# Two attention layers with a feed-forward: rests of two chunk pairs issued together, and another order of the first projections

## The chip, the cores and the metric

The kernel runs on one core of a Trainium2 chip, in one launch. The metric is the device time of that launch in microseconds, the median of the runs shown; lower is better. Engines: TensorE (PE; its weight loads are listed apart as PEld), VectorE (DVE), ScalarE (ACT), GpSimd (POOL) and SyncE (SP), which here only issues transfers.

## The reference

Two layers over x of 4 x 512 x 320 (batch, rows, features), with a context of 4 x 1601 x 192. Each layer is self-attention with 20 heads of 16, cross-attention to the context, and a gated feed-forward, all in fp32:

```python
h1 = _ln(x, n1_g, n1_b)
x = _attn(h1, h1, q1, k1, v1, o1_w, o1_b, heads) + x
h2 = _ln(x, n2_g, n2_b)
x = _attn(h2, context, q2, k2, v2, o2_w, o2_b, heads) + x
h3 = _ln(x, n3_g, n3_b)
proj = h3 @ ff_w1 + ff_b1
a, g = jnp.split(proj, 2, axis=-1)
ff = a * jax.nn.gelu(g, approximate=False) @ ff_w2 + ff_b2
return ff + x
```

`ff_w1` is 320 x 2560, `ff_w2` 1280 x 320.

## The kernel before

**Units.** The work is a list of units in a fixed order: for each layer, self-attention for every batch and each of five groups of four heads, the same for cross-attention, then one feed-forward unit per batch. There are 88 units, eight of them feed-forward (here counted 0 to 7 in their order: 0 to 3 in the first layer, 4 to 7 in the second). The kernel writes out its own order (`manual_schedule`): each engine runs its instructions in the order in which the Python code issues them, and waits on semaphores for data and for buffers.

**Side work.** Everything that is not a unit's own main work (projections of queries, keys and values for units to come, norms, output projections) lies as closures in chains with a cost and a due round. `steps` runs some of them at fixed points of the main work; `run(chain)` runs the head of one chain at once, `until(test, chain)` runs heads until the test holds. The maxima of a later unit's scores (`max_pairs`: two score matmuls, then a VectorE reduction) are given out in the same way by `giver`.

**PSUM.** There are eight banks: pool `ps_st` has four single banks (tag `st`), pool `ps_m` two double ones (tag `m`). Side work takes a single bank (`step_bank`, L337), except in the opening, where it takes a double one. A set of four maxima in the opening and in a feed-forward unit takes one double bank and two single ones (`banks`, L879 to L886).

**Feed-forward unit** (`ff_main`, L1158). The normed and transposed x (`hT`) has 320 features: two slabs of 128 and a rest of 64. The 1280 hidden features are ten chunks of 128. For a chunk, the value half (index 0) and the gate half (index 1) each need two full matmuls over 128 rows (`full`, L1182) and one over the 64 rows left (`rest`, L1194). The 64 rows are stored twice, so that the rest of the value half uses the upper 64 rows of the array and the rest of the gate half the lower 64, side by side. `gate` is a Gelu on ScalarE (L1200) and one VectorE operation (L1201). Chunks go in pairs: side work (`beside`), four full matmuls of the first chunk, side work, four of the second, then the four rests of both, then the two gates. A pair holds two single banks and one double bank. After the five pairs, the second product (`yps`, L1221) follows with four row tiles, each over ten chunks.

**Opening** (L1341 to L1377). Unit 0's norm is made, then the queries and keys of units 0 and 1 are projected (`queries`, L687; `keys`, L713). Each projection is twelve matmuls into one bank. For unit 0, ScalarE (L631) and VectorE (L629) put the bank into the head slots by turns; for all others ScalarE copies it (`qst`, `kst`) and GpSimd puts it into slots (L635). Then four rounds of unit 0's maxima follow (sps L891, reduced at L907), with one piece of unit 0's values (`vps`, L818) between two rounds. There are eight pieces of values: four for the first two groups, four for the others. After the maxima come unit 2's queries, a piece of values, `max_reduce` and `max_end` (the maxima are turned and sent into the query buffer by eight small transfers, L962, from SP, ScalarE and GpSimd), loads, unit 2's keys and three pieces of values. Then the main loop starts with unit 0's scores (`st`, L1062).

Of the kernel before, what the change touches and what calls it, by code (L numbers as in the profile page):

```python
# [9 lines left out]
F32 = mybir.dt.float32  # L10
# [9 lines left out]
FF = 4 * D  # L20
L = 2
EPS = 1e-5
P = 128
# [20 lines left out]
NHC = FF // P  # L44
# [4 lines left out]
FK = [(0, 0, P), (1, P, P)]  # L49
REST = D - 2 * P  # L50
# [16 lines left out]
def kernel(ctx: ExitStack, tc: tile.TileContext, x, context, ws, out):  # L67
# [18 lines left out]
    nc = tc.nc  # L86
# [9 lines left out]
    ps_st = ctx.enter_context(tc.tile_pool(name="ps_st", bufs=4, space=PSUM))  # L96
    ps_m = ctx.enter_context(tc.tile_pool(name="ps_m", bufs=2, space=PSUM))
# [8 lines left out]
    for b in range(2):  # L106
        k, o = (const.tile([P, 1], F32, name=f"{n}{b}") for n in ("keep", "ones"))
# [11 lines left out]
    for i in range(2):  # L119
        m = const.tile([P, SLOT], F32, name=f"nmax{i}")  # L120
# [25 lines left out]
    for b in range(2):  # L146
        k = const.tile([P, 1], F32, name=f"kept{b}")
# [5 lines left out]
    for b in range(2):  # L153
        rows = slice(b * GD, (b + 1) * GD)
# [20 lines left out]
    w1 = wpool.tile([P, 2, 2 * FF], F32, name="w1")  # L175
# [6 lines left out]
    w1r = wpool.tile([P, FF], F32, name="w1r")  # L182
# [121 lines left out]
    at = 0  # L304
# [23 lines left out]
    chains = {n: deque() for n in ("divide", "project", "slots", "norm", "context", "early", "proj", "values")}  # L328
# [6 lines left out]
    start = {"on": True, "both": False}  # L335

    def step_bank(shape, name):  # L337

        if start["on"] and start["both"]:
            return ps_m.tile([P, 2, 512], F32, tag="m", name=name)[:, 0]  # L340
        return ps_st.tile(shape, F32, tag="st", name=name)

    def warm(n):

        ps = step_bank([P, 512], "wps")
        for _ in range(n):
            nc.tensor.matmul(ps[:, : 4 * P], lhsT=ident, rhs=fill, start=True, stop=True)
# [4 lines left out]
    def add(chain, cost, f, due, ready=yes, soon=yes):  # L352
        chains[chain].append((cost if isinstance(cost, tuple) else (cost,), due, ready, soon, f))
# [15 lines left out]
    def run(chain):  # L369
        costs, _, ready, _, f = chains[chain].popleft()  # L370
        assert ready(), chain
        f()
        clock["credit"] -= sum(costs)
# [49 lines left out]
    def until(test, name):  # L423
        while not test():
            assert chains[name], name
            run(name)
# [210 lines left out]
    def add_proj(u):  # L637
        wq, wk = wq2 if u.cross else wq1, wk1
        chain = "early" if u.early else "proj"
# [13 lines left out]
        first = units[u.i - u.g]  # L653
# [27 lines left out]
        def queries(part):  # L681
            w = N // 2 // parts
            at = [i * (N // 2) + part * w for i in range(2)]
            ps = step_bank([P, 512], "qps")
            for k, _, n in DK:
                for i, to, gs in tiles:
                    nc.tensor.matmul(  # L687
                        ps[to, :w],
                        lhsT=wq[:n, k, gs],
                        rhs=first.hT[:n, k, at[i] : at[i] + w],  # L690
                        start=(k == 0),
                        stop=(k == 2),
                    )
            if u.i == 0:
                for i in range(2):
                    to_slots(u.qbuf, at[i], ps, w, i, False, kept)
            else:
                stage = two.tile([P, N // 2], F32, tag="stage", name="qst")
                nc.scalar.mul(stage[:, :w], ps[:, :w], DH**-0.5)  # L699
                for i in range(2):  # L700
                    to_slots(u.qbuf, at[i], stage, w, i, False)
            if part == parts - 1:
                u.q = u.qbuf
                first.made["q"] += 1
                u.qwhen = -9 if start["on"] else clock["round"]
# [73 lines left out]
        def add_queries():  # L779
            if u.g == 0 and u.cross:  # L780
                add(chain, 0.0, hold, due - 4, yes, lambda: "h" in u.own)
            for part in range(parts):
                add(chain, (0.05 + 0.427 / parts,) * 3, lambda part=part: queries(part), due - 2, unread)

        if not u.cross:
            add_queries()
            add(chain, (0.477,) * 3, keys, due, free)
        else:
            add(chain, 2.45, keys_of_context, keys_due, free)
            add_queries()  # L790
            for _ in range(HG):
                add(
                    "slots", 0.0, lambda: u.kslots and u.kslots.popleft()(), keys_due,
                    lambda: u.keyed, lambda: clock["slots"] > 0,
                )
# [149 lines left out]
    def max_reduce(u):  # L945
        if u.pm is not None:
            nc.vector.tensor_reduce(
                u.nm[:, : HG * NQ].rearrange("p (j t) -> p t j", t=NQ), u.pm, AX.X, ALU.max, negate=True
            )
# [97 lines left out]
    def round_of(scores, maxima):  # L1047

        then = [f() for f in scores] + [f() for f in maxima]
        for f in then:  # L1050
            f()
# [106 lines left out]
    def ff_main(u, give, nxt):  # L1158
        done = 0

        def beside(room, n):

            nonlocal done
            if room:
                for extra in give(done, True)[1]:
                    round_of([], extra)
            done += n
            if done == u.steps - 1 and nxt is not None and nxt.kind != "ff":
                max_reduce(nxt)
                max_end(nxt)  # L1170
            steps(True)
            for _ in range(n - 1):
                steps(False)

        hc = one.tile([P, 6, N], F32, tag="ctxT", name="hid")
        hid = [hc[:, i, :] for i in range(6)]

        hid += [kbuf[1][:, i * N : (i + 1) * N] for i in range(3)] + [kbuf[2][:, :N]]

        def full(c, i, ps):  # L1180
            for k, at, n in FK:
                nc.tensor.matmul(  # L1182
                    ps,
                    lhsT=w1[:, k, i * FF + c * P : i * FF + (c + 1) * P],
                    rhs=u.hT[:, k, :],
                    start=(k == 0),
                    stop=False,
                )
            return ps

        def rest(c, pss):
            for i, ps in enumerate(pss):
                rows = slice(i * REST, (i + 1) * REST)
                nc.tensor.matmul(  # L1194
                    ps, lhsT=w1r[rows, c * P : (c + 1) * P], rhs=u.hT[rows, 2, :], start=False, stop=True
                )

        def gate(c, pss):
            gl = prs.tile([P, N], F32, tag="pr", name="gl")
            nc.scalar.activation(gl, pss[1], AF.Gelu, bias=b1[:, NHC + c : NHC + c + 1])  # L1200
            nc.vector.scalar_tensor_tensor(hid[c], pss[0], b1[:, c : c + 1], gl, ALU.add, ALU.mult)  # L1201

        for c in range(0, NHC, 2):

            beside(True, 2)
            gates = ps_m.tile([P, 2, 512], F32, tag="m", name="fps")
            pss = []
            for i in range(2):
                if i:
                    beside(False, 2)  # L1210
                ps = ps_st.tile([P, 512], F32, tag="st", name="fps")
                pss.append([full(c + i, 0, ps), full(c + i, 1, gates[:, i])])
            for i in range(2):
                rest(c + i, pss[i])
            for i in range(2):
                gate(c + i, pss[i])
        ff_read.append(u)
        for t in range(NQ):
            ps = ps_st.tile([P, 512], F32, tag="st", name="yps")
            for c in range(NHC):  # L1220
                nc.tensor.matmul(  # L1221
                    ps[:, :D],
                    lhsT=hid[c][:, t * P : (t + 1) * P],
                    rhs=w2[:, c, :],
                    start=(c == 0),
                    stop=(c == NHC - 1),
                )
            nc.vector.tensor_tensor(xs[u.b][:, t, :], ps[:, :D], xs[u.b][:, t, :], ALU.add)
            if u.l == L - 1:
                dma(out=out[u.b, t * P : (t + 1) * P, :], in_=xs[u.b][:, t, :])  # L1230
            beside(True, 1)
        after(u)
# [35 lines left out]
    def left(v):  # L1268
        return sum(map(len, v.pairs))
# [75 lines left out]

    add_norms(0)
    add_proj(units[0])
    warm(5)
    add_proj(units[1])
    until(lambda: not chains["proj"], "proj")  # L1350
    add_values(units[0])
    add_proj(units[2])
    first = units[0]
    first.pairs = max_pairs(first)
    start["both"] = True
    while left(first):
        round_of([], first.pairs[0].popleft() + first.pairs[1].popleft())
        if left(first):
            run("values")

    run("proj")
    run("values")
# [9 lines left out]
    start["on"] = start["both"] = False  # L1372
    run("proj")

    for _ in range(3):
        run("values")
    clock["credit"] = 0.0  # L1377

# [45 lines left out]
```

## Time and profile before

| | |
|---|---|
| median of 3 runs | 3214.34 us (3212.0 to 3215.55) |
| profiled execution | 3212.79 us |
| span of its trace | 3211.0 us |
| granted TensorE clock, mean | 0.999 |

Busy time in us by stage, from the trace. The two feed-forward stages are the third and the fifth row.

| stage, us from the start | PE | DVE | ACT | POOL |
|---|---|---|---|---|
| opening, 0 to 34 | 28.30 | 20.53 | 8.52 | 18.45 |
| attention, layer 0, 34 to 1334 | 1285.00 | 963.40 | 942.21 | 564.10 |
| feed-forward, layer 0, 1334 to 1633 | 295.50 | 75.81 | 38.03 | 41.50 |
| attention, layer 1, 1633 to 2934 | 1288.80 | 947.07 | 944.33 | 559.98 |
| feed-forward, layer 1, 2934 to 3211 | 273.07 | 56.06 | 32.96 | 19.09 |

A row of the timeline gives the start, the busy time from first to last, the engine and source line, the operation, output and inputs by their names in the program (with buffer numbers left out), the sizes, and the count; in brackets stands how long the engine had been idle and what ended that. Adjacent instructions of one line are merged into one row. The profile counts two TensorE instructions (passes) for each matmul of the program. Ends of matmuls are modelled; the distances between starts are the safer reading.

### The profile page before, as it was taken

Reading aid. Unit: us, or ns where it says so; the run is one execution under the profiler, and the core shown is the slowest. Engines: PE = TensorE matmul, PEld = TensorE weight load, DVE = VectorE, ACT = ScalarE, POOL = GpSimd, SP = SyncE. Lnnn points to the kernel's source line nnn. Section 1 sums busy time; section 2 is a strip of 40 time slices with the busy share of each in tenths; the row PEclk is TensorE's granted clock in tenths of the full one; section 3 lists DMA queues with packets and bytes.
Section 4 is the critical chain, followed back from the end, with each engine's and each line's share of the span. In section 5 each row is a group of like instructions: output and inputs, shape, how many; then the busy total and the mean of one; then the engine's idle time right before and its main releaser. Section 6 shows DMA issues by size and latency. Waiting matters only on the chain.

```text
span 3211.0 us, 81827 instructions
## 1 busy us (share of the span) xinstructions
PE 3170.7 (99%) x33970; PEld 1465.7 (46%) x33970; DVE 2062.9 (64%) x2663; ACT 1966.1 (61%) x3951; POOL 1203.1 (37%) x1617
## 2 busy tenths in 40 slices
PE   9999999999999999999999999999999999999999
PEld 3444444444444444354444444444444444443555
DVE  7776877778778677422247778777777777773221
ACT  4666577777777777611146665777778777785110
POOL 4555234444443443211225553344444444442000
PEclk9999999999999999999999999999999999999999
DMA  2130011100100100100012100010010010001000
GB/s 67 48 78 17 14 24 40 33 21 19 33 21 20 31 16 11 39 6 0 1 30 56 38 14 14 21 29 16 16 31 11 16 33 10 15 10 37 9 11 15
DMA packets 104999, 77.94 MB, mean 24 GB/s; under 512 B 42924, under 2 KB 95156, under 8 KB 104628
## 3 DMA queue, kind: packets, MB, share of 16 engines
q1 hardware_dynamic: 104544, 72.70, 9.3%
q8 instruction: 268, 4.39, 0.6%
q14 instruction: 103, 0.84, 0.1%
q0 software_dynamic: 64, 0.00, 0.0%
q10 hardware_dynamic: 20, 0.00, 0.0%
HBM read 33.04 MB, written 7.93 MB: 13 GB/s over the span
## 4 chain that ended last, share of the span: by engine, by line
PE 63%; DVE 2%; POOL 1%; ACT 0%; issue 0%; DMA 0%; SPq 0%; POOLq 0%; DVEq 0%
PE st L1062 15%; PE av L1082 13%; PE fps L1182 9%; PE sps L891 8%; PE yps L1221 5%; PE fps L1194 2%; PE ops L1009 2%; PE kps L743 2%; PE qps L687 2%; PE vps L836 2%; PE sps L915 1%; PE vps L818 1%; PE kps L713 1%; PE hps L489 1%; DVE nmax L907 1%; DVE pm L907 1%
## 5 line engine op out<-in xcount | busy, mean ns | idle before, releaser
L1068 ACT ACTIVATE pr<-st 128x512 f32<-128x512 f32 (+1 forms) x2720 | 1412.7, 601 | 432.1 <-PE sps L891 349.0
L1062 PE MATMUL st<-q,kT 32*128 32x512 f32 (+1 forms) x5440 | 1374.4, 615 | 9.7 <-ACT pr L1068 5.7
L907 DVE TENSOR_REDUCE pm<-sps 128x2 f32<-128x1024 f32 (+1 forms) x974 | 1134.8, 1203 | 271.9 <-PE sps L891 265.8
L891 PE MATMUL sps<-kT,q 32*128 32x512 f32 x5120 | 1272.6, 620 | 14.3 <-DVE nmax L907 11.7
L1099 POOL TENSOR_TENSOR o<-o,vo 128x512 f32<-128x512 f32 x576 | 736.2, 1278 | 1389.0 <-ACT vo L1098 1248.3
L1062 PEld LDWEIGHTS st<-q,kT 32*128 32x128 f32 (+1 forms) x5440 | 511.3, 181 | 528.0 <-ACT pr L1068 309.3
L1082 PE MATMUL av<-pr,vals 128*32 128x512 f32 (+1 forms) x5440 | 730.4, 605 | 0.2
L907 DVE TENSOR_REDUCE nmax<-sps 128x2 f32<-128x1024 f32 (+1 forms) x339 | 378.4, 1157 | 155.9 <-PE sps L891 152.8
L891 PEld LDWEIGHTS sps<-kT,q 32*128 32x128 f32 x5120 | 408.5, 183 | 120.7 <-issue 79.3
L1098 ACT COPY vo<-av 128x512 f32<-128x512 f32 x576 | 347.4, 603 | 41.8 <-PE av L1082 37.8
L1082 PEld LDWEIGHTS av<-pr,vals 128*32 128x32 f32 (+1 forms) x5440 | 109.9, 108 | 495.3 <-ACT pr L1068 483.5
L1182 PE MATMUL fps<-hT,w 128*128 128x512 f32 x640 | 288.2, 599 | 1.1 <-DVE hid L1201 0.6
L1200 ACT ACTIVATE gl<-fps,b 128x512 f32<-128x512 f32 x80 | 50.7, 684 | 387.4 <-PE fps L1194 387.3
L635 POOL TENSOR_SCALAR q<-qst,keep,zero 64x128 f32<-64x128 f32 (+1 forms) x476 | 230.4, 484 | 48.6 <-ACT qst L699 15.4
L1182 PEld LDWEIGHTS fps<-hT,w 128*128 128x128 f32 x640 | 117.3, 190 | 148.6 <-issue 143.2
L1201 DVE SCALAR_TENSOR_TENSOR hid<-fps,b,gl 128x512 f32<-128x512 f32 x48 | 33.8, 746 | 163.1 <-ACT gl L1200 163.1
L1009 PEld LDWEIGHTS ops<-wo,aT 112*32 112x32 f32 (+1 forms) x3072 | 97.7, 110 | 68.4 <-issue 37.6
L687 PE MATMUL qps<-hT,wq 112*32 112x128 f32 (+3 forms) x2880 | 125.6, 308 | 0.5 <-DVE pm L907 0.5
L1009 PE MATMUL ops<-wo,aT 112*32 112x160 f32 (+1 forms) x3072 | 125.2, 300 | 0.2
L687 PEld LDWEIGHTS qps<-hT,wq 112*32 112x32 f32 (+1 forms) x2880 | 86.2, 110 | 79.0 <-issue 38.0
L437 POOL TENSOR_SCALAR root<-root 128x4 f32<-128x4 f32 x23 | 5.3, 230 | 309.4 <-DVE root L431 308.8
L502 POOL TENSOR_TENSOR x<-x,brow 128x320 f32<-128x320 f32 x96 | 84.0, 893 | 89.1 <-DVE hn L476 78.3
(88 smaller groups left out, 2182.4 us busy)
## 6 DMA issues: line engine op xcount, KB each, us to landing
kT<-kst SPq DMA_DIRECT2D x320, 48.0 KB
aT<-o SPq DMA_DIRECT2D x320, 32.0 KB
q<-turned SPq DMA_DIRECT2D x636, 1.0 KB
w<-in_L_xattn_ff_w_dram SPq DMA_DIRECT2D x20, 256.0 KB
ctxT<-ctxT SPq DMA_DIRECT2D x24, 208.0 KB
ctxT<-ctxT SPq DMA_DIRECT2D x12, 416.0 KB
ctxin<-in_ctx_dram SPq DMA_DIRECT2D x24, 192.0 KB
w<-in_L_xattn_ff_w_dram SPq DMA_DIRECT2D x20, 160.0 KB
```

Of the source, the lines that this page charges most:

```text
L635: nc.gpsimd.tensor_scalar(to, stage[rows, :w], keep[b][rows], more[rows], ALU.mult, ALU.add)
L687: nc.tensor.matmul(ps[to, :w], lhsT=wq[:n, k, gs], rhs=first.hT[:n, k, at[i] : at[i] + w], start=(k == 0), stop=(k == 2),)
L891: nc.tensor.matmul(ps, lhsT=u.q[j * SLOT : (j + 1) * SLOT, t * P : (t + 1) * P], rhs=u.kT[j * SLOT : (j + 1) * SLOT, u.k0 + s * 512 : u.k0 ...
L907: nc.vector.tensor_reduce(to[:, j : j + n], part, AX.X, ALU.max, negate=(ns == 1))
L1009: nc.tensor.matmul(ps[f : f + m, : D // 2], lhsT=aT[:n, k, t * P + f : t * P + f + m], rhs=wo[:n, k, cols], start=(k == 0), stop=(k == 2),)
L1062: nc.tensor.matmul(st[:r, :], lhsT=u.kT[rows, u.k0 + u.cols[c] : u.k0 + u.cols[c] + r], rhs=u.q[rows, :], start=True, stop=True)
L1068: nc.scalar.activation(p[:r], st[:r], AF.Exp)
L1082: nc.tensor.matmul(ps[i * SLOT : (i + 1) * SLOT, :], lhsT=columns_of[:r, head : head + SLOT], rhs=pr.pop((c, j))[:r, :], start=True, stop= ...
L1098: nc.scalar.copy(vo, ps)
L1099: nc.gpsimd.tensor_tensor(u.o, u.o, vo, ALU.add)
L1182: nc.tensor.matmul(ps, lhsT=w1[:, k, i * FF + c * P : i * FF + (c + 1) * P], rhs=u.hT[:, k, :], start=(k == 0), stop=False,)
L1221: nc.tensor.matmul(ps[:, :D], lhsT=hid[c][:, t * P : (t + 1) * P], rhs=w2[:, c, :], start=(c == 0), stop=(c == NHC - 1),)
```

## The change

There are three edits.

1. In `ff_main`, `rest` becomes `rests`, for a whole pair of chunks, and can come first or last. When a pair has not been begun ahead, its full matmuls run as before, then its rests, and directly behind them the banks of the next pair are taken and that pair's rests are issued, as the first matmuls of their sums (`start=True`). The gates of the first pair follow. The next pair then has only its full matmuls, the last of which closes the sums. With five pairs in a unit, pairs 1 and 3 are begun ahead; pair 4 is as before. The side work keeps its places: two points per pair.
2. In `add_proj`, unit 0's keys are added ahead of its queries; for all other units the order stays.
3. In the opening, unit 0's projections alone come before its maxima; unit 1's queries stand after the first round of maxima, its keys after the second, a piece of values after the third. After unit 2's keys, four pieces of values follow instead of three.

Apart from the rests, the opening and the work in it that these edits move, the instructions of every engine stand in the order of before. SP's and GpSimd's order does not change at all.

```diff
         if not u.cross:
-            add_queries()
+            if u.i:
+                add_queries()
             add(chain, (0.477,) * 3, keys, due, free)
+            if not u.i:
+                add_queries()
...
+        def full(c, pss, ahead):
+
             for i, ps in enumerate(pss):
+                for k, at, n in FK:
+                    nc.tensor.matmul(
+                        ps,
+                        lhsT=w1[:, k, i * FF + c * P : i * FF + (c + 1) * P],
+                        rhs=u.hT[:, k, :],
+                        start=ahead and k == 0,
+                        stop=not ahead and k == 1,
+                    )
+
+        def rests(c, pss, ahead):
+
+            for e in range(2):
+                for i, ps in enumerate(pss[e]):
+                    rows = slice(i * REST, (i + 1) * REST)
+                    nc.tensor.matmul(
+                        ps,
+                        lhsT=w1r[rows, (c + e) * P : (c + e + 1) * P],
+                        rhs=u.hT[rows, 2, :],
+                        start=ahead,
+                        stop=not ahead,
+                    )
...
+        def banks():
+            gates = ps_m.tile([P, 2, 512], F32, tag="m", name="fps")
+            return [[ps_st.tile([P, 512], F32, tag="st", name="fps"), gates[:, e]] for e in range(2)]
+
+
+        pss = None
         for c in range(0, NHC, 2):
...
+            ahead = pss is not None
+            if not ahead:
+                beside(True, 2)
+                pss = banks()
+
+            for e in range(2):
+                if e or ahead:
+                    beside(ahead and not e, 2)
+                full(c + e, pss[e], not ahead)
+            these, pss = pss, None
+            if not ahead:
+                rests(c, these, False)
+                if c + 2 < NHC:
+                    pss = banks()
+                    rests(c + 2, pss, True)
+            for e in range(2):
+                gate(c + e, these[e])
...
     warm(5)
+    until(lambda: not chains["proj"], "proj")
     add_proj(units[1])
-    until(lambda: not chains["proj"], "proj")
     add_values(units[0])
     add_proj(units[2])
     first = units[0]
     first.pairs = max_pairs(first)
     start["both"] = True
-    while left(first):
+    for chain in ("proj", "proj", "values", None):
         round_of([], first.pairs[0].popleft() + first.pairs[1].popleft())
-        if left(first):
-            run("values")
+        if chain:
+            run(chain)
...
-    for _ in range(3):
+    for _ in range(4):
         run("values")
```

More of the change, by code (lines that the diff above doesn't have):

```diff
@@ L1178, in ff_main @@
         hid += [kbuf[1][:, i * N : (i + 1) * N] for i in range(3)] + [kbuf[2][:, :N]]
[L1180 to L1191, printed above, removed]
-            for i, ps in enumerate(pss):
[L1193 to L1196, printed above, removed]
+        def full(c, pss, ahead):
+            for i, ps in enumerate(pss):
+                for k, at, n in FK:
[17 more added lines that the diff above has]
+                    )
         def gate(c, pss):
@@ L1201, in gate @@
             nc.vector.scalar_tensor_tensor(hid[c], pss[0], b1[:, c : c + 1], gl, ALU.add, ALU.mult)
+        def banks():
+            gates = ps_m.tile([P, 2, 512], F32, tag="m", name="fps")
+            return [[ps_st.tile([P, 512], F32, tag="st", name="fps"), gates[:, e]] for e in range(2)]
+        pss = None
         for c in range(0, NHC, 2):
[L1205 to L1216, printed above, removed]
+            ahead = pss is not None
[14 more added lines that the diff above has]
+                gate(c + e, these[e])
         ff_read.append(u)
```

## The prediction

> **What bounds the kernel.** I read the page's totals first, then the TensorE stream of the feed-forward stages in order of time, then the first 35 us on all engines.
>
> ```profile
> span 3211.0 us, 81827 instructions
> PE 3170.7 (99%) x33970; PEld 1465.7 (46%) x33970; DVE 2062.9 (64%) x2663; ACT 1966.1 (61%) x3951; POOL 1203.1 (37%) x1617
> PEclk9999999999999999999999999999999999999999
> ```
>
> TensorE is busy 3170.7 of 3211.0 us at the full clock. No work on it is removed: the built order of the changed program holds the same matmuls, and outside the start and the eight feed-forward units the order on every engine is as before. So the change can act only through what lies between matmuls: the price of switching between shapes, waits for a PSUM bank, and the start, where TensorE is not yet the bound.
>
> **The price of a switch.** The last feed-forward unit has nothing beside it (TensorE in order of time: start, duration, line):
>
> ```profile
> 3149.91 7.13 PE L1182 MATMUL fps<-hT,w 128*128 128x512 f32 x16
> 3156.98 1.99 PE L1194 MATMUL fps<-hT,w1r 64*128 64x512 f32 x8
> 3158.89 7.13 PE L1182 MATMUL fps<-hT,w 128*128 128x512 f32 x16
> ```
>
> The profile shows two passes per matmul. Rows of L1182 with 8 and 16 passes last 3.70 and 7.13 us elsewhere, so a pass takes 3.43 / 8 = 0.429 us. L1194's two 64-row halves run side by side: 8 passes count as 4. A period is 3158.89 - 3149.91 = 8.98 us, and 20 x 0.429 = 8.57; the 0.41 left is two switches, **0.205 us each**. A switch hides nothing and is hidden by nothing while TensorE is the bound.
>
> **Part 1, the rests.** Before, every pair of chunks runs F8 R4 (8 full matmuls, 4 rests), with other work before the first and between the two F4. After, pairs 1 and 3 of a unit (counted from 0) have their rests run directly behind those of pairs 0 and 2: R8, later F8 with no R4. Counted in the two built orders, switches from a unit's first L1182 to its last rest and the work behind it are, unit by unit, 18, 11, 10, 26, 18, 13, 10, 10 before (116) and 15, 7, 6, 24, 15, 10, 6, 6 after (89). 27 x 0.205 = **-5.5 us**.
>
> [...] The row is of this very switch, so I take -5.5.
>
> **What the open pair costs.** [...] There are four single banks and two double ones; a pair holds two singles and a double, so at R8 two open pairs hold all. Work directly behind R8 must wait for the gates of the first. [...] The rows give the price (VectorE, ScalarE, TensorE around one rest of unit 3):
>
> ```profile
> 1584.59 1.99 PE L1194 MATMUL fps<-hT,w1r 64*128 64x512 f32 x8
> 1586.65 1.27 ACT L1200 ACTIVATE gl<-fps,b 128x512 f32<-128x512 f32 x2 [5.09 <-PE fps L1194]
> 1587.37 1.41 DVE L1201 SCALAR_TENSOR_TENSOR hid<-fps,b,gl 128x512 f32<-128x512 f32 x2 [9.37 <-ACT gl L1200]
> 1588.17 0.86 PE L818 MATMUL vps<-wv,hT 112*32 112x128 f32 x24 [0.53 <-DVE hid L1201]
> 1588.69 2.41 DVE L907 TENSOR_REDUCE nmax<-sps 128x2 f32<-128x1024 f32 x3
> ```
>
> Let R be the start of the rests. The Gelu starts at R + 2.06, and a matmul that waits for the first gate's bank starts at R + 3.58 (1588.17 - 1584.59). The second bank comes one gate, 0.67, later: R + 4.25. R8 itself lasts 8 x 0.429 + 0.205 = 3.63. So whoever needs one bank finds it free (3.58 < 3.63): **0** for five of the nine (output projections, keys, a lone transpose), with 0.05 to spare. The built order's waits show ScalarE released by the fourth rest, not the eighth.
>
> At one place in unit 3, three banks are asked for: R8, maxima (sps), then values (vps), where the values' only bank is the one a maximum has just been written to. VectorE must finish both gates (R + 4.2), then reduce the double bank, whose scores start at R + 3.63 and are readable about 1.25 later as at the start (17.74 to 18.99), so R + 4.88; plus 1.2 and 0.6 (the 2.41 row is 1.2 + 0.6 + 0.6) and a 0.07 release: values at R + 6.75. Before they stood at R + 3.58; adding the 1.71 of the four extra rests gives 5.29. **+1.5 us**. Queued behind that wait on TensorE is everything; nobody else is late.
>
> At three places the three transposes of the next norm (hps) stand behind a rest, and before, the third of them or the full matmuls behind already wait for the first gate:
>
> ```profile
> 1435.44 1.99 PE L1194 MATMUL fps<-hT,w1r 64*128 64x512 f32 x8
> 1437.36 1.09 PE L489 MATMUL hps<-ident,hn 128*128 128x128 f32 x8
> 1439.03 0.66 PE L489 MATMUL hps<-ident,hn 128*128 128x128 f32 x4 [0.58 <-DVE hid L1201]
> 1439.52 7.10 PE L1182 MATMUL fps<-hT,w 128*128 128x512 f32 x16
> ```
>
> From rest to full matmul that is 4.08. After: first transpose at R + 3.63, second at 4.25 (second gate), third when ScalarE has copied the first (after both Gelus; 0.72 a copy): about 5.0, full matmuls at 5.5. Less the 1.71 moved in: 3.8, a gain of 0.3 in units 1 and 2. In unit 6 (rest at 3097.41, full matmuls at 3101.00: 3.59) only two transposes follow: 4.25 + 0.49 - 1.71 = 3.0, a gain of 0.55. Together **-1.15**.
>
> Where R8 is followed by F (unit 7, and the first R8 of most), the banks are held already and nothing waits. Part 1: -5.5 + 1.5 - 1.15 = **-5.15 us**.
>
> **Part 2, the start.** TensorE is idle for long here; the end is set by evacuations, then by maxima on VectorE, then by small transfers:
>
> ```profile
> 17.13 0.55 DVE L629 TENSOR_SCALAR kT<-kps,keep,ones 64x256 f32<-64x256 f32 x1 [0.63 <-ACT kT L631]
> ...
> 17.74 1.24 PE L891 MATMUL sps<-kT,q 32*128 32x512 f32 x8 [0.30 <-DVE kT L629]
> ...
> 18.99 9.78 DVE L907 TENSOR_REDUCE nmax<-sps 128x2 f32<-128x1024 f32 x12 [1.30 <-PE sps L891]
> ...
> 30.80 1.30 POOL L962 DMA_DIRECT2D q<-turned  x2
> ...
> 34.08 0.70 PE L1062 MATMUL st<-q,kT 32*128 32x512 f32 x2 [1.35 <-ACT vals L825]
> ```
>
> ScalarE and VectorE empty two banks, queries then keys, each in four alternating steps (13.61 to 17.68 us, a step every 0.58). The first maxima need all keys but only the first half of the queries. With keys first, the last two steps are no longer waited for: 17.74 - 2 x 0.58 = 16.57. VectorE's own last step still ends at 17.68, just ahead of the first scores at 16.57 + 1.25 = 17.82. Unit 1's projections, 24 passes each (L687 and L713 take 1.3 to 1.45), had cost nothing before: they ran under the evacuations. Now they stand between the maxima, 1.43 + 1.17 for the scores = 2.60 against VectorE's 2.45 (9.78 / 4): 0.15 lost twice. The values they displace (0.86) fitted. So the last maximum ends 1.17 - 0.3 = **0.9** earlier. From there on all is queued as before: POOL copies unit 2's queries (2.48) ahead of its two transfers, which the first scores at 34.08 wait for, and both hang on the query projection behind the last maxima: it moves with them. The four values then behind the keys take at most 2 x 0.8 + 2 x 1.0, ending before 33. The sixth values now stand among unit 2's maxima, where VectorE works without a pause (9.53 us in 11 reductions from 40.93): 0; if TensorE were the bound there, +1.0. SP's transfers keep their order. **-0.9 us**, from -1.2 to +0.1.
>
> **Sum.** -5.15 - 0.9 = -6.05 on the profiled execution: 3212.79 to 3206.7 with the span from 3211.0 to 3205.0. Its own time lies 1.55 below the median; on the median, 3214.34 - 6.1 = **3208.2**.
>
> **Rivals.**
> - The gates come later than the rows say (slower). If ScalarE were released only when all eight rests are through, each of the nine places pays 1.7 more: 15.4 - 6.1 = +9.3, **3223.6**. It decides from 0.7 us a place (6.1 / 9). For it: 3.58 against 3.63 is a margin of 0.05, and at unit 3 one wait is real. Against: the wait is on the fourth rest. 0.08.
> - The start gives nothing and the edges cost a little more (0.1 at each of the nine): -6.1 + 0.9 + 0.9 = -4.3, **3210.0**. For it: the first scores wait for a chain that includes POOL and transfers. 0.24.
> - More is gained: the wait in unit 3 is not met, because the values find another bank: -7.6, **3206.7**. Against it: the waits of the built program. 0.18.
> - That the change does not do what it says is excluded by the built order.
>
> My forecast has 0.50, with 3206.5 to 3210 around it.
>
> **Range and chances.** Down to the larger gain with the start at its best (3214.34 - 7.9 = 3206.4), less 1.8 for the scatter of the three runs shown (3212.0 to 3215.55): 3204.6. Up to the smaller gain plus 1.8: 3212. Less than 0.2%, 6.4 us, is about what a measurement of this kernel cannot tell from no change, so the line lies at 3207.9, just under my forecast. Faster: the larger gain (0.18) and a little over half of the forecast (0.28), 0.46. Same: the rest of the forecast (0.22) and the smaller gain (0.24), 0.46. Slower: 0.08.
>
> **What would show it.** Right: in the last unit, rests of 16 passes whose successor starts 3.63 us later, and three of them instead of five; a wait of about 1.5 us before the values in unit 3, and none of note behind the other R8; the first maxima at 17.8 and the first scores at 33.1; the two feed-forward stages shorter by 5 us together. Wrong: waits for a gate of 0.5 us or more behind most R8, a first score still near 34, or a gain that turns up in the attention stages, which nothing here touches.

## The result, and the profile after

| | before | after |
|---|---|---|
| median | 3213.99 us (22 runs, 3210.83 to 3218.35) | 3208.68 us (22 runs, 3205.31 to 3212.6) |
| ratio, 95% interval | | 0.9982 (0.9975 to 0.9988) |
| span of the profiled execution | 3211.0 us | 3209.2 us |
| granted TensorE clock, mean | 0.999 | 0.997 |

The change takes 5.3 us off (3.9 to 8.0 by the interval). The prediction's sum was 6.05, and its time 3208.2.

The page of the changed kernel has as many instructions as before on every engine, and nearly the same busy time of TensorE (busy us, share of the span, instructions):

```profile
PE 3170.0 (99%) x33970; PEld 1470.0 (46%) x33970; DVE 2064.1 (64%) x2663; ACT 1965.7 (61%) x3951; POOL 1201.8 (37%) x1617
```

The two profiled spans differ by only 1.8 us. Where the other 3.5 went is seen by stage, with a second profile of the changed kernel (after_again, below) beside the first. Each boundary is the start of a TensorE row: the first scores, the first full matmul of a feed-forward stage, the first scores of layer 1.

| stage, us | before | after | after_again |
|---|---|---|---|
| opening | 34.08 | 33.42 | 31.87 |
| attention, layer 0 | 1300.00 | 1298.86 | 1298.79 |
| feed-forward, layer 0 | 301.74 | 301.74 | 301.73 |
| attention, layer 1 | 1292.56 | 1295.90 | 1295.75 |
| feed-forward, layer 1 | 282.62 | 279.28 | 279.26 |

Feed-forward of layer 1 is 3.34 shorter. That of layer 0 has not changed at all. The opening differs by 1.55 between two executions of the same program. And the attention of layer 1, which the change doesn't touch, is 3.34 and 3.19 longer in the two profiles of it. The rows explain each.

**Layer 1.** The last unit on TensorE (start, duration, line, sizes, passes):

```profile
3146.98 3.70 PE L1200 MATMUL fps<-hT,w1r 64*128 64x512 f32 x16
3150.61 14.00 PE L1187 MATMUL fps<-hT,w 128*128 128x512 f32 x32
3164.54 3.70 PE L1200 MATMUL fps<-hT,w1r 64*128 64x512 f32 x16
```

The rests come as 16 passes, their successor 3.63 later, and nothing waits: two pairs cost one stretch of rests instead of two.

**The open pair.** In unit 1 the transposes behind the rests are released nearly as forecast (TensorE):

```profile
1432.70 3.70 PE L1200 MATMUL fps<-hT,w1r 64*128 64x512 f32 x16
1436.34 1.27 PE L489 MATMUL hps<-ident,hn 128*128 128x128 f32 x8
1437.87 0.66 PE L489 MATMUL hps<-ident,hn 128*128 128x128 f32 x4 [0.26 <-ACT hT L496]
```

The full matmuls follow at 1438.36, which is 3.95 behind the rests without the 1.71 of the four rests moved in (forecast 3.8, before 4.08). Only the third transpose shows a wait, 0.26, for ScalarE's copy of the first.

Unit 3 is where layer 0 loses again what it gains:

```profile
1579.99 3.70 PE L1200 MATMUL fps<-hT,w1r 64*128 64x512 f32 x16
1583.62 1.73 PE L894 MATMUL sps<-kT,q 32*128 32x512 f32 x8
1586.68 0.86 PE L821 MATMUL vps<-wv,hT 112*32 112x128 f32 x24 [1.32 <-DVE nmax L910]
1587.47 5.35 PE L1187 MATMUL fps<-hT,w 128*128 128x512 f32 x8
```

The values stand at R + 6.69 (forecast R + 6.75), behind the wait for the maximum that was foreseen. Then comes what was not: the next eight full passes take 5.35 instead of 3.70. The windows of 5 us (busy time by engine, then the granted clock, the DMA share and GB/s) show why:

```profile
1585.00:1590.00 5.00, 3.68 (x28) 1.77 (x28) 3.36 (x7) 0.27 (x1) 0.00 (x0) 0.74 0.02 3
1590.00:1595.00 5.00, 5.00 (x32) 2.08 (x31) 0.00 (x0) 0.37 (x1) 0.13 (x1) 0.92 0.00 0
```

The clock fell, to 0.74 and 0.92 as means of these windows. The trace's own record of the clock has it at 0.50 for 3.41 us, from 1587.42 on. Half of that, 1.71, is about the 1.65 that the eight passes lose.

**The opening** of the profiled run has the same loss. TensorE, VectorE and GpSimd in order:

```profile
16.55 1.42 PE L894 MATMUL sps<-kT,q 32*128 32x512 f32 x8 [1.71 <-DVE q L629]
17.90 2.79 PE L687 MATMUL qps<-hT,wq 112*32 112x256 f32 x24
18.06 2.42 DVE L910 TENSOR_REDUCE nmax<-sps 128x2 f32<-128x1024 f32 x3 [0.38 <-PE sps L894]
...
21.82 7.37 DVE L910 TENSOR_REDUCE nmax<-sps 128x2 f32<-128x1024 f32 x9 [1.34 <-PE sps L894]
...
31.22 1.30 POOL L965 DMA_DIRECT2D q<-turned  x2
...
33.42 0.70 PE L1065 MATMUL st<-q,kT 32*128 32x512 f32 x2
```

The first scores for the maxima start at 16.55 (forecast 16.57). The clock record has the next fall from 17.29 on, and unit 1's queries take 2.79 instead of 1.50, so VectorE waits 1.34 for its second round, and the maxima end at 29.19: 0.4 later than before, not 0.9 earlier. Still the first score is 0.66 earlier, since it now comes 2.20 behind GpSimd's transfers, and came 3.28 behind them (34.08 - 30.80). So one loss was not foreseen (the clock), and one gain (the transfers).

### The profile page after: what moved, and what is told of

Read it like the earlier page. It is cut to its first block, busy times and chain, and to the rows that moved or that the text cites. A ratio compares the mean times of both kernels' runs of the same rounds, so it can differ in the third digit from the quotient of the medians.

```text
span 3209.2 us, 81827 instructions
## 1 busy us (share of the span) xinstructions
PE 3170.0 (99%) x33970; PEld 1470.0 (46%) x33970; DVE 2064.1 (64%) x2663; ACT 1965.7 (61%) x3951; POOL 1201.8 (37%) x1617
## 3 DMA queue, kind: packets, MB, share of 16 engines
q8 instruction: 268, 4.39, 0.6%
## 4 chain that ended last, share of the span: by engine, by line
PE 64%; DVE 2%; POOL 1%; ACT 0%; issue 0%; DMA 0%; SPq 0%; POOLq 0%; DVEq 0%
PE st L1065 16%; PE av L1085 13%; PE fps L1187 9%; PE sps L894 8%; PE yps L1241 5%; PE fps L1200 2%; PE ops L1012 2%; PE kps L743 2%; PE qps L687 2%; PE vps L839 2%; PE sps L918 1%; PE hps L489 1%; PE vps L821 1%; PE kps L713 1%; DVE nmax L910 1%; DVE pm L910 1%
```

## The experiments

**The two halves alone.** `rests_only` has the new feed-forward and the old opening; `start_only` the reverse. The edits are the two halves of the change's diff; of the second:

```diff
+    until(lambda: not chains["proj"], "proj")
     add_proj(units[1])
...
-    while left(first):
+    for chain in ("proj", "proj", "values", None):
```

> The rests of two pairs together, the opening as before. Theory (27 switches fewer at 0.205 us, 1.15 gained at the transposes, 1.5 lost at the bank wait in unit 3 and 1.7 more there because the clock falls to half for one window of 3.4 us after that wait): -5.5 - 1.15 + 1.5 + 1.7 = -3.5 us against the kernel before. Rival (the clock's fall in unit 3 was chance): -5.2. Rival (the gain of the whole change comes from the opening): 0. The trace should show the values in unit 3 about 6.7 us after the rests, and full matmuls behind them at 5.3 us for 8 passes if the fall belongs to the wait, 3.7 if it was chance.

> The new opening, the feed-forward as before. Theory (the gap of 1.7 us before the first maxima halves TensorE's clock for one window, which eats 1.4 of what keys first gain): -0.7 to -1.5 us against the kernel before, with the query projection of unit 1 again at about 2.8 us instead of 1.5. Rival (the fall in the opening was chance): -2, the projection at 1.5, the last maximum at about 27.8. Rival (the opening carries the gain of the whole change): -5.

Measured: `rests_only` 3209.69 (21 runs), ratio 0.9991 (0.9984 to 0.9997), 3.8 below the median of before; `start_only` 3212.23 (13 runs), ratio 0.9993 (0.9985 to 1.0001), 1.2 below. Together -5.0, against -5.3 for the whole: the halves add up, and neither is nothing, though for `start_only` alone the interval reaches just past 1. In `rests_only` unit 3 shows the same wait of 1.32, and the clock falls there too: behind it the values take 1.21 instead of 0.86, and the eight full passes 5.00 instead of 3.70.

**The rests of unit 3 left as before, the rest of the change kept.**

```diff
-                if c + 2 < NHC:
+                if c + 2 < NHC and (nxt is None or nxt.kind == "ff"):
```

`nxt` is the unit behind; only unit 3 has an attention unit there.

> The whole change, but in feed-forward unit 3, the one with maxima beside it, every pair is as before. Theory: the bank wait of 1.5 and the fall of the clock (1.7) go, two switches (0.4) come back: 2.8 us faster than the whole change, so about -8 against the kernel before, and unit 3 lasts 63.6 us from its first transpose to the second product instead of 66.1. Rival (that wait costs nothing in the end, because the attention units behind make it up): as the whole change, -5.3.

Measured: 3204.97 (7 runs), ratio 0.9973 (0.9962 to 0.9985): 8.5 below the kernel before as measured beside it; the change was 5.3 below. In unit 3 the rests start at 1579.91 and the values 3.59 later, as before (TensorE):

```profile
1583.50 0.87 PE L821 MATMUL vps<-wv,hT 112*32 112x128 f32 x24 [0.53 <-DVE hid L1211]
1584.29 3.70 PE L1187 MATMUL fps<-hT,w 128*128 128x512 f32 x8
```

The feed-forward of layer 0 is 299.18 instead of 301.74, 2.56 shorter. So reordering unit 3, which saves two switches, costs 2.56 net where the clock falls.

**Two dummy matmuls in the gap before the first maxima.**

```diff
     start["both"] = True
+    warm(2)
```

> The whole change, with two more matmuls of no use (identity by a constant tile, 4 passes, 1.7 us) put into the gap before the first maxima; nothing else is altered. Theory (idle TensorE halves its own clock): unit 1's query projection takes 1.5 us instead of 2.8, the maxima end at 27.8 instead of 29.2, the first scores stand 1.4 earlier: 1.4 us faster than the whole change, -6.7 against the kernel before. Rival (the projection is slow for another reason, say an operand that comes late): no faster, or 0.2 slower for the added passes.

In its opening the dummies run from 14.57 to 16.55; behind the first scores come (TensorE and VectorE):

```profile
17.55 1.51 PE L687 MATMUL qps<-hT,wq 112*32 112x256 f32 x24
17.73 9.84 DVE L910 TENSOR_REDUCE nmax<-sps 128x2 f32<-128x1024 f32 x12 [0.26 <-PE sps L894]
```

With the gap filled the queries take 1.51 and the twelve reductions run through; the first score is at 31.80, 1.62 earlier than in the change's first profile. The time is 3208.09 (12 runs), ratio 0.9983 (0.9975 to 0.9992): 5.4 below before where 6.7 was expected, and no different from the change. Its profile gives a second reading that was not planned: unit 3 has the same wait of 1.32, and no fall behind it.

```profile
1585.06 0.86 PE L821 MATMUL vps<-wv,hT 112*32 112x128 f32 x24 [1.32 <-DVE nmax L910]
1585.85 3.70 PE L1187 MATMUL fps<-hT,w 128*128 128x512 f32 x8
```

Its layer-0 feed-forward is 300.08: the wait alone costs 300.08 - 299.18 = 0.90, the fall 301.74 - 300.08 = 1.66.

**The change again**, for a second profile.

> The change itself once more, for a second profile and beside the other three on one chip. Theory (a fall of the clock follows a gap of TensorE of 1.3 to 1.7 us, if the gap and the windows of the clock lie so that enough of one window is idle): the opening's fall is there again between 15 and 25 us; the fall in unit 3 behind the 1.32 wait is there or not. Time -5.3 against before, as in the first comparison; u3_warm 4 less than it. Rival (the falls are chance, wherever they come): no fall in the opening.

Measured: 3208.76 (16 runs), ratio 0.9983 (0.9976 to 0.9991). In the opening the rival was right, for this execution: the same gap, no fall, and maxima without a pause from 17.80 to 27.64 (TensorE and VectorE):

```profile
16.55 1.14 PE L894 MATMUL sps<-kT,q 32*128 32x512 f32 x8 [1.71 <-DVE q L629]
17.62 1.50 PE L687 MATMUL qps<-hT,wq 112*32 112x256 f32 x24
17.80 9.84 DVE L910 TENSOR_REDUCE nmax<-sps 128x2 f32<-128x1024 f32 x12
```

In unit 3 the clock fell, as in the first profile. Counted over the profiles that have the bare gap of 1.71 in the opening, it fell in three of six (`after`, `start_only`, `no_ahead_u3`; not in `after_again`, `no_ahead_again`, `fetch_after`); behind unit 3's 1.32 in three of five (`after`, `after_again`, `rests_only`; not in `warm_gap`, `fetch_after`). Whether it comes differs from one execution to the next; the last section shows from the clock records what decides it at these two places.

**Both losses mended**, with dummies, or with work that is needed anyway in the gap:

```diff
     start["both"] = True
-    for chain in ("proj", "proj", "values", None):
+    run("values")
+    for chain in ("proj", "proj", None, None):
```

> The whole change, with unit 3 left in the old order of rests (as in no_ahead_u3), and two matmuls on numbers that nobody reads in the gap before the first maxima (as in warm_gap). Theory (two separate losses of the change, each mended by itself): 1.6 less than no_ahead_u3 in its profile at the first score, so about 3203.5 where no_ahead_u3 gave 3205.0, and some -9.5 to -10 against before. Rival (the clock fall in the opening only moves: the windows of the clock run on, and a fall saved here comes elsewhere): the same as no_ahead_u3, -8.5. Rival (the gap of unit 3 was chance in one run of rounds): as warm_gap, -5.4.

> As u3_warm, but what fills the gap before the first maxima is work that is needed anyway: the first piece of unit 0's values comes there, instead of between the third and the fourth round of the maxima. Theory (the clock falls because TensorE stands still for 1.7 us): the piece fills about 0.9 to 1.3 of the gap, no fall, TensorE's queue behind it is 0.9 shorter than in u3_warm, but the maxima are VectorE's and end at the same time or 0.3 later, since VectorE or another engine copies the piece out; so first score at 31.8 to 32.4 and the time within 0.6 of u3_warm. Rival (a gap of 0.5 to 0.8 that stays is enough for a fall): maxima at half speed as in the change, first score at 33.1 to 33.6, the time that of no_ahead_u3.

Measured: `u3_warm` 3206.49 (9 runs), ratio 0.9975 (0.9965 to 0.9984); `u3_values` 3204.82 (7 runs), ratio 0.9974 (0.9963 to 0.9984). No gain over `no_ahead_u3` is seen, though the first score in these two profiles is at 31.80 and 31.54 instead of 33.08. In those profiles the clock fell twice in the attention of layer 0, in that of `no_ahead_u3` once. Once more, on one chip:

> The change with unit 3 left in the old order (as no_ahead_u3), once more for a narrower interval, beside the next kernel. Theory (the loss of unit 3 is 0.9 in the wait and 1.7 in a fall of the clock behind it, in some 3 of 5 executions): 0.9973 again, 2 to 3.5 better than the change's 0.9982; the bare gap of 1.7 us in the opening brings a fall or not. Rival (the first seven runs were lucky): 0.998 to 0.9985.

> The same with a piece of values in the gap before the first maxima (as u3_values), once more. Theory (the filled gap saves a fall worth 1.55 in some 3 of 5 executions, and falls elsewhere are chance): about 1 us less than no_ahead_again. Rival (a fall saved in the opening comes at one of the later standstills instead): the same time within the interval.

Measured: 3207.06 (5 runs), ratio 0.9965 (0.9953 to 0.9978), and 3206.37 (6 runs), ratio 0.9967 (0.9955 to 0.9979). The runs of the kernel before fell into two groups here, around 3213 and 3220, so these ratios support the first ones and don't sharpen them; the two kernels beside each other can't be told apart. The filled gap buys nothing that these runs can measure. Whether a fall saved in the opening comes later, or the saving is lost in the scatter of chance falls, is open.

**The price of a switch, by a dose the other way.** In the kernel before, each chunk's rests directly behind its own full matmuls: 69 switches more.

```diff
                 pss.append([full(c + i, 0, ps), full(c + i, 1, gates[:, i])])
-            for i in range(2):
                 rest(c + i, pss[i])
```

> The kernel before, with the rests of a chunk issued right behind that chunk's own four full matmuls instead of one stretch for the pair. Nothing else is changed. A feed-forward unit then switches more often between full passes and passes of 64 rows: 185 switches in the eight units instead of 116, 69 more. [...] Against it stands that the first chunk's gate starts four full matmuls earlier, so that the edge waits at the banks of the units with side work, 0.5 to 0.6 each, may shrink by up to 3.3. So +9 to +14, likeliest +11. Rival (a switch costs nothing, and the gain of the rests in the change came from the gates' timing): earlier gates, so 0 or down to -3. Rival (the price is only paid on one edge of a stretch of rests): +5 to +7.

Measured: 3227.68 (5 runs), ratio 1.0043 (1.0030 to 1.0055), 14.1 above before. The last unit:

```profile
3156.43 3.70 PE L1182 MATMUL fps<-hT,w 128*128 128x512 f32 x8
3160.07 1.13 PE L1194 MATMUL fps<-hT,w1r 64*128 64x512 f32 x4
3161.12 3.70 PE L1182 MATMUL fps<-hT,w 128*128 128x512 f32 x8
```

A chunk takes 3161.12 - 3156.43 = 4.69, a pair 9.38, against 8.98 in the kernel before: 0.40 for two switches more. From the first full matmul of a stage to the scores behind it (layer 0), or to the last row of the second product (layer 1), the stages are 6.46 and 7.04 longer, 13.50 / 69 = 0.196 a switch. Rivals of nothing and of one edge alone fall. The edge waits gave back much less than the 3.3 allowed for them.

**The transfers.** What made them land sooner in the new opening? The rate of all DMA from 27 to 36 us, in 40 slices of 0.225 us, first in the kernel before, then in the changed one:

```profile
GB/s 0 0 0 0 0 0 0 0 0 0 0 0 0 0 5 0 5 0 5 1 76 5 5 5 1 17 114 182 336 86 51 119 267 359 336 330 171 250 232 241
```

```profile
GB/s 0 0 0 0 0 0 0 0 0 73 0 0 0 0 0 0 5 2 2 0 5 3 1 5 5 5 0 40 165 239 279 245 370 319 347 256 262 234 180 174
```

The peak that stands alone (76, 73) is a fetch of 16 KB of instructions. The profile's page counts 268 on that queue, 4.39 MB, one for every 127 of TensorE's 33970 passes, or 254 instructions with the weight load of each pass (127 is the count where the expectation of `fetch_before` says 128). Whose instructions they are is read by stage: in the kernel before, the four stages behind the opening have 123, 10, 124 and 8 fetches, one for 127, 131, 126 and 129 passes of TensorE, but for 16, 6, 15 and 6 instructions of ScalarE and 10, 17, 9 and 16 of VectorE. So they are taken for TensorE's. Before, the lone fetch lies at 31.5 us, inside the flight of GpSimd's transfers (issued at 30.80); after, at 29.0, ahead of it. That suggested a test: more but narrower dummy matmuls at the very start move every fetch 27 matmuls forward in the work. In the old opening this takes a fetch out of the flight; in the new one it brings the next fetch in.

```diff
-    warm(5)
+    warm(32, 76)
```

> The kernel before; only the five dummy matmuls of 512 columns at the very start are 32 of 76 columns, about as long together. TensorE's instruction stream has 27 matmuls more, so each fetch of its instructions (one for every 128 passes, 16 KB) comes 27 matmuls earlier in the work. Before, a fetch lay at 31.5 us, inside the flight of GpSimd's two small transfers (issued at 30.80, landed 2.9 us later). Theory (a fetch of TensorE's instructions in that flight holds the transfers up by about 1 us): the fetch now comes at about 29, ahead of the flight; issue to landing 1.9 instead of 2.9, first score 1.0 earlier against the end of the maxima (4.2 to 4.3 us behind it instead of 5.3), time about -1. Rival (the flight is shorter with the new order for another reason, the state of SP's queue or of the copies): 2.9 to 3.5 as in all profiles of the old opening.

> The whole change with the same 32 narrow dummy matmuls. In the change the fetches lay at 29.0 and 35.25 us and the flight from 31.2 to 33.1, with none inside. 27 matmuls earlier puts the second of them at about 32, inside the flight. Theory: issue to landing 2.9 to 3.5 instead of 1.9, and the first score 1 us later against the end of the maxima (5.2 instead of 4.2). Rival: 1.9 as in all profiles of the new opening. The clock may fall or not behind the 1.7 gap, so distances are read from the end of the maxima, not from the start.

The narrow dummies lasted 13.91 us instead of 7.27, so both openings are some 6 us late as a whole, and the times (3219.86, ratio 1.0014, 1.0007 to 1.0021; and 3216.32, ratio 1.0001, 0.9993 to 1.0009) say nothing on this. GpSimd's row among the DMA issues (count, size, median us from issue to landing) in `fetch_before`:

```profile
q<-turned POOLq DMA_DIRECT2D x2, 1.0 KB, 2.0
```

and in `fetch_after`:

```profile
q<-turned POOLq DMA_DIRECT2D x2, 1.0 KB, 2.5
```

Both moved the way the theory said, `fetch_before` to the forecast 2.0, `fetch_after` to 2.5, short of the 2.9 to 3.5 that were forecast. The profiles read for it, with the fetch's slice from GpSimd's issue:

| profile | fetch, us from the issue | landed after, us |
|---|---|---|
| before | +0.75 | 2.9 |
| split_rests | +1.0 | 3.0 |
| rests_only | +1.5 | 3.5 |
| fetch_after | +0.25 | 2.5 |
| fetch_before | -1.75 | 2.0 |
| after, after_again, start_only, no_ahead_u3 | -2.25 | 1.9 |
| warm_gap, u3_warm | -2.0 | 1.9, 2.0 |
| u3_values | -1.25 | 1.7 |

In the four profiles with a fetch inside the flight, the transfers land 2.0 to 2.25 behind it. From the end of the maxima to the first score it is 5.31 before and 3.93 in `fetch_before`, 4.23 in the change and 4.88 in `fetch_after` (forecast 5.2).

## Why the prediction was right

**Switches, -5.5.** Right. By the dose, 27 x 0.196 = 5.3; layer 1 has 14 fewer and none of unit 3's losses, and by the forecast's terms 14 x 0.205 and 0.55 for unit 6's transposes make -3.4 there: it gave -3.34. The runs bear out the row's price of 0.205: as an estimate from it, 69 x 0.205 = 14.1 for the dose, measured 13.5 in the two stages. No run shows the smaller price behind +9, the lower end of what was forecast for `split_rests`: it was 0.196 a switch there, and 14.1 in all.

**Transposes, -1.15.** Right in kind, a little too large: in units 1 and 2 the distance from rest to full matmul shrank by 4.08 - 3.95 = 0.13 each, not 0.3; in unit 6 it is 3.03, forecast 3.0. That makes -0.8. Units 1 and 2 as a whole gave -1.00 and -1.02, forecast 4 x 0.205 + 0.3 = -1.12 each.

**Room behind the open pair.** The nine places are those where other work stands behind R8 (units 0 to 6: 1, 2, 1, 2, 1, 1, 1). Zero at those with one bank, 1.5 at unit 3: right, with the margin of 0.05 that the first rival doubted. For unit 3 as a whole +1.5 - 0.41 = +1.1 was forecast, and the wait alone gives +0.90. What the prediction put at nothing is what follows: a fall of the clock, +1.66 more in three of five profiles. It gave the wait no price beyond its length.

**The opening, -0.9.** About right as a sum (-1.2 for `start_only`), wrong in its parts. Where the clock stays up (`after_again`) the maxima end at 27.64, 1.13 earlier, so the 0.15 that was to be lost twice between them did not appear; and the first score is 2.21 earlier, not 0.9, because the step "from there on all is queued as before" failed. The same transfers were issued in the same order, but no longer met a fetch of TensorE's instructions: from the end of the maxima to the first score it is 4.23 instead of 5.31, worth another 1.1. Where the clock falls behind the gap of 1.71, 1.55 of that is lost again. The gap is the change's own: unit 1's projections used to stand in it. The prediction called them free and asked only what they cost between the maxima, not what their leaving does to TensorE.

**The sum.** Without falls the four terms read from traces are -3.34 (layer 1), -2.56 (units 0 to 2), +0.90 (unit 3) and -2.21 (opening): -7.2. Half a fall at each of the two new standstills gives back about 1.6, so -5.6, beside -5.3 measured. That the time came out so near is in part luck: two things left out, a gain of 1.1 and losses of 1.6 on average, nearly cancel. The sign that the two feed-forward stages would be 5 us shorter together holds only without the fall in unit 3: -3.34 and -1.66 make -5.00, with the stage of `warm_gap`; in both profiles of the change it is -3.34. The attention stages differ by falls elsewhere, as the last section shows.

**What would beat it.** The change without unit 3, 3204.97 at ratio 0.9973, is the version that the runs support. Its interval overlaps that of the change (0.9975 to 0.9988), but all five comparisons of kernels with unit 3 in the old order lie at 0.9975 or below, the three of the change and of `warm_gap` at 0.9982 or 0.9983, and the trace shows the 2.56. A filled gap in the opening on top of it has not been shown to help.

## What to carry to other kernels

Count the switches between shapes of matmul in the built order and take their price from a stretch with nothing else in it; here it held within 5% (0.205 from the row, 0.196 from the dose). When work is moved out of a wait, ask what the engine does there now: a wait of TensorE may cost its own length and then a stretch at half clock (here 0.90 and 1.66 us in unit 3). And an end that hangs on small transfers can move by a microsecond through the place of an instruction fetch (here 1.9 us from issue to landing without one in the flight, 2.9 with one), so such a gain belongs to this exact instruction stream and may be gone with the next edit.

## What the hardware showed that was not expected

**Short standstills can halve the clock.** In twelve profiles (before, after and all experiments but the last two) every fall of the clock (to 0.50, for 3.41 us) but one lay behind a standstill of TensorE of 0.84 to 1.81 us, of which a profile has about a dozen. (The fall at the very end, where TensorE has no more work, is not counted.) The one left (`rests_only` at 50) lay behind two of 0.35 and 0.59. Most standstills are the same in all profiles, and the fall comes in some: behind the one near 133 us (1.23 to 1.27) in seven of the twelve, near 225 (0.84 to 0.89) in five, near 370 (1.34) in none.

The clock records of the traces show what decides it at the change's two places. In all fourteen profiles together there are 42 falls. Each starts a whole number of periods of 3.413 us after the clock's first rise, to within 0.003 us, and lasts one period. Where the program lies on this grid differs from one execution to the next (the first rise is at 8.01 us in the trace of before, at 7.05 in the change's first). The longest part of the standstill that lay within one period, in us:

| standstill | profiles with a fall behind it | profiles without |
|---|---|---|
| opening, 1.71 | 1.71, 1.71, 1.71 | 1.61, 0.96, 0.94 |
| unit 3, 1.32 | 1.32, 1.32, 1.32 | 0.93, 0.77 |

The fall came where one period held the whole standstill, and not where a boundary cut it. If every place on the grid is equally likely, an estimate from these lengths is (3.41 - 1.71) / 3.41 = 0.5 and (3.41 - 1.32) / 3.41 = 0.6 of the executions. Elsewhere the whole standstill in one period is not enough: the one near 370 lay so in six profiles and brought no fall. What else counts, these runs don't tell.

The clock goes with the scatter too: the 22 runs of the change lie at 3205.3 to 3205.8 where the mean clock is 0.999, 3207.3 to 3209.4 at 0.998, and 3210.1 to 3212.6 at 0.997. Its two profiles happen to have two falls each in the attention of layer 1 (near 1738 and 1830), before has none: that is the 3.2 to 3.3 us in a stage that the change doesn't touch.

**An instruction fetch of TensorE holds up GpSimd's transfers,** by 0.6 to 1.6 us in the four profiles where one fell into their flight. The traces' records of single DMA packets show part of how. Without a fetch in the flight, all 32 packets of the first transfer start in a group, 1.3 us behind the issue. With one, two of the 32 are missing from the group: in `fetch_after` they start at 38.33 and 38.34, and the fetch lasts from 37.04 to 38.29. So two packets seem to stand behind the fetch. The landing then comes 1.05 behind them, where it comes 0.5 behind the group without a fetch; why is open.
